# Feature-major float16 halves of both FFNs' routing: from TensorE transposes and two PSUM copies to transposing transfers on SyncE's queue

## The chip, the cores and the metric

The kernel runs on one NeuronCore of a Trainium2 chip. The metric is device time in microseconds (us) of one execution. The kernel before took 2360.64 us (median of three runs: 2363.73, 2360.64, 2348.91). Below, PE is TensorE, PEld its weight load, DVE is VectorE, ACT is ScalarE, POOL is GpSimd, and SP is SyncE, which computes nothing and issues transfers. "DMA share" is the mean busy share of the core's 16 DMA engines.

## The reference

The input `x` has 2 sequences of 4096 tokens with 512 features. Three layers follow one another: half an FFN, an attention layer with a delta-rule state, and the same FFN again with the same weights. Only the FFN's routing matters here:

```python
x = x + 0.5 * ffn(layernorm(x), ...)
x = x + attn(layernorm(x), ...)
x = x + 0.5 * ffn(layernorm(x), ...)

# ffn, on the normalised x
ctx = concatenate([x, broadcast(slot_mean)], axis=-1)
h = gelu(ctx @ w1.T + b1, approximate=False)            # 256 hidden features
route_logits = (h @ w2.T + b2) / (abs(tau) + 0.1)       # 64 slots
topk_vals, topk_idx = top_k(route_logits, 8)
alpha = softmax of the 8 kept logits, 0 elsewhere       # token x slot
slot_input = einsum('bts,btd->bsd', alpha, x)
...                                                     # a GRU step on the slots
out = einsum('bts,bsd->btd', alpha, slot_values) @ wo.T + bo
```

A product on PE contracts over partitions. So `ctx @ w1.T` needs the normalised `x` with features on the partitions (feature-major), while the layer norm makes it with tokens on the partitions, and the slot sum wants tokens on the partitions.

## The kernel before, in words

The program has five stretches: routing of the first FFN (phase "a", tiles whose names end in `a`), its GRU step, attention (the long middle), routing of the second FFN (phase "c"), and the last GRU step with the output. Both routings run the same function, `ffn_a_phase` (line 309).

A block is 128 tokens of both sequences (`NB` = 2, written `b`), so there are 32 blocks. Blocks are put in groups of four (the first, and the last few, in smaller ones). Each group goes through six generators, and `run_merged` (line 60) deals them out by a due time that each `yield` gives, in units of groups. The order that this makes is what the Tile framework starts from when it fixes each engine's own order; at run time each engine, SP among them, runs its instructions in that order and waits at one until what it depends on is done. The generators are:

- `a_load` (line 349) starts the load of a block's `x`, 512 KB, on SP's queue, 1.4 groups ahead. Phase a has 7 buffers `xt` for it, phase c has 4, and 12 blocks kept in tiles `kx` for the end.
- `a_stats` (line 355): mean and variance on DVE (`bn_stats`, line 361).
- `a_norm` (line 368): DVE writes the normalised block `fxn` (line 379, 2 buffers); ACT rounds it to float16, `xh` (line 383); POOL takes the rest, `xl = fxn - xh`, in float16 (line 385). The pair keeps the product close to float32. Then both halves are made feature-major: for each, PE makes 8 transposes of 128x128 (line 394, tile `fpt`) into a PSUM tile, and ACT (for `xh`, line 397) or DVE (for `xl`, line 399) copies that to `fxTh` or `fxTl` in SBUF, 3 buffers each. The PSUM tiles come from the pool `ptr` (tag `tr`, 3 buffers), which other users share.
- `a_hidden` (line 402), due 0.44 groups (1.76 blocks) after the norm of the same block: 24 matmuls on PE through `mm3` (lines 128 to 130: `fxTh` by the high half of w1, `fxTh` by its low half, `fxTl` by the high half), tile `fph`, then Gelu on ACT (line 417, tile `hT`) and the logits on PE (line 421, tile `pl`).
- `a_topk` (line 425), once for a group, nearly all on DVE: the eight largest logits, the softmax, and the two float16 halves `ahl` of alpha.
- `a_slots` (line 463): PE transposes alpha (tile `fpa`, line 472), ACT copies it out (line 579 in phase a, from where SP stores it to `ald` at line 580; line 595 in phase c), and PE adds up the slots from `xh`, `xl` and `ahl` (lines 480 to 482, tile `sl`). So `xh` and `xl` stay alive until then (10 or 11 buffers).

Phase a also prepares attention's weights in between: their loads are on SP's queue, their splitting is on DVE and ACT (line 176 and 177), and 96 matmuls are on PE (line 248). SP's queue holds, in phase a, the loads `xt`, the weight loads and the stores `ald`; in phase c the loads of `xt` and `kx`, and the weights of the GRU step.

Of the kernel before, what the change touches and what calls it, by code (L numbers as in the profile page):

```python
# [11 lines left out]
F16 = mybir.dt.float16  # L12
# [7 lines left out]
P = 128  # L20
D = 512
KC = D // P
# [5 lines left out]
NB = 2  # L28
# [66 lines left out]
def tile_macaron(  # L95
# [7 lines left out]
    nc = tc.nc  # L103
    V = nc.vector
# [30 lines left out]
    ident16 = cp.tile([P, P], F16, tag="ident16", name="ident16")  # L135
# [173 lines left out]
    def ffn_a_phase(load, adst, nm, extra, before=None, after=None):  # L309

        with tc.tile_pool(name=f"sl{nm}", bufs=1, space=PSUM) as slp, tc.tile_pool(name=f"gp{nm}", bufs=1) as gp:
# [3 lines left out]
            with tc.tile_pool(name=f"f{nm}", bufs=2) as wp, tc.tile_pool(name=f"fs{nm}", bufs=2) as sm, \  # L315
                    tc.tile_pool(name=f"ft{nm}", bufs=3, space=PSUM) as ptr, \
                    tc.tile_pool(name=f"fp{nm}", bufs=2, space=PSUM) as ppj, \
                    tc.tile_pool(name=f"fl{nm}", bufs=2, space=PSUM) as ppl:
                groups = split_blocks(NBLK)
                ng = len(groups)  # L320
                pools = (wp, sm, ptr, ppj, ppl)
                st = [dict() for _ in range(ng)]
                items = []
                for g, (b0, n) in enumerate(groups):
                    args = (st[g], nm, g, (b0, n), pools)
                    t0, t1 = b0 / GB, (b0 + n) / GB
                    items += [
                        (t0 - PA["ld"] - n / GB, t1 - PA["ld"] - n / GB, lambda a=args: a_load(*a, load)),
                        (t0 - PA["st"], t0 - PA["st"] + PA["std"], lambda a=args: a_stats(*a)),
                        (t0, t1, lambda a=args: a_norm(*a)),  # L330
                        (t0 + PA["a2"], t1 + PA["a2"], lambda a=args: a_hidden(*a)),
                        (t1 + PA["a2"], t1 + PA["tk"], lambda a=args: a_topk(*a, wacc)),
                        (t1 + PA["tk"], t1 + PA["tk"] + PA["sl"] * n / GB, lambda a=args: a_slots(*a, adst, sl, ng)),
                    ]
                items += extra(gp, ptr, gw, NBLK / GB)
                run_merged(items)
                for i in range(1, GB):
                    nc.gpsimd.tensor_tensor(wacc[:, 0:NB], wacc[:, 0:NB], wacc[:, NB * i:NB * i + NB], ALU.add)
# [29 lines left out]
    def a_norm(d, nm, gi, blocks, pools):  # L368

        wp, sm, ptr, ppj, ppl = pools  # L370
        mv, rs = d["mv"], d["rs"]
        d["xhl"], d["xT"] = [], []
        for j in range(blocks[1]):
            u = f"{nm}{gi}_{j}"
            xs = d["x"][j]
            xn = wp.tile([P, NB, D], F32, tag="xn", name=f"fxn{u}", bufs=CFG[nm]["XN"])
            for b in range(NB):
                i = NB * j + b
                V.tensor_scalar(xn[:, b], xs[:, b], mv[:, i, 0:1], rs[:, i:i + 1], ALU.subtract, ALU.mult)
            xh = wp.tile([P, NB, D], F16, tag="xh16", name=f"xh{u}", bufs=CFG[nm]["XH"])  # L380
            xl = wp.tile([P, NB, D], F16, tag="xl16", name=f"xl{u}", bufs=CFG[nm]["XH"])
            d["xhl"].append((xh, xl))
            nc.scalar.copy(xh, xn)
            yield (j + 0.2) / blocks[1]
            nc.gpsimd.tensor_tensor(xl, xn, xh, ALU.subtract)
            yield (j + 0.4) / blocks[1]
            xTh = wp.tile([P, KC, NB * P], F16, tag="xTh", name=f"fxTh{u}", bufs=3)
            xTl = wp.tile([P, KC, NB * P], F16, tag="xTl", name=f"fxTl{u}", bufs=3)
            d["xT"].append((xTh, xTl))
            for src16, dst, eng in ((xh, xTh, 0), (xl, xTl, 1)):  # L390
                pt = ptr.tile([P, KC, NB * P], F16, tag="tr", name=f"fpt{u}_{eng}")
                for k in range(KC):
                    for b in range(NB):
                        nc.tensor.transpose(pt[:, k, b * P:(b + 1) * P], src16[:, b, k * P:(k + 1) * P], ident16)
                    yield (j + 0.4 + 0.3 * eng + 0.07 * (k + 1)) / blocks[1]
                if eng == 0:
                    nc.scalar.copy(dst, pt)
                else:
                    V.tensor_copy(dst, pt)
                yield (j + 0.7 + 0.3 * eng) / blocks[1]  # L400

    def a_hidden(d, nm, gi, blocks, pools):

# [764 lines left out]
```

## Time and profile before

One profiled execution took 2342.8 us, of which 2341.0 us are the span from its first instruction to its last, at a mean granted TensorE clock of 0.960. It is 18 us under the median of the three timed runs.

| what | value |
|---|---|
| DVE, busy of the span | 1911.3 us (82%) |
| ACT, busy of the span | 1148.9 us (49%) |
| POOL, busy of the span | 808.5 us (35%) |
| first and last `bn_stats` of phase a | 16.0 and 208.4 us |
| first transpose `fpt` and last slot matmul of phase a | 26.2 and 273.8 us |
| first transpose `fpt` and last slot matmul of phase c | 2019.6 and 2250.0 us |
| transfers issued by SP in phase a, one `xt` load | 512 KB, median 0.38 us of SP's time |

The engines' busy times lie side by side, so they are not added up. A stretch is set by the engine that is busy nearly all of it, or by a chain of waits where none is. How much an instruction costs is seen from its duration only on DVE, ACT and POOL; matmuls overlap in the pipeline, and what counts there is how far apart they start.

### The profile page before, as it was taken

The page shows a single profiled execution, that of the slowest core. Times are in us where ns is not written, and L with a number is a line of the kernel's source. Part 1 is how long each engine was busy: PE and PEld are TensorE (multiplying, and loading weights), DVE is VectorE, ACT ScalarE, POOL GpSimd, SP SyncE. Part 2 cuts the span into 40 slices and gives each one's busy share as a digit, 9 for nine tenths or more (in the row PEclk, how much of TensorE's full clock was granted, in tenths as well). Part 3 has the DMA queues.
Part 4 walks back from the last instruction along what each step waited for, and adds up shares of the span by engine and source line. Part 5 has one row for each costly group of instructions (what it writes and reads, how often), then busy time and mean ns, then how long its engine had stood idle before and what let it go on. Part 6 is the DMA issues. An engine that isn't in the chain of part 4 may idle for free. (4 is left out here: it accounts for less than half of the span.)

```text
span 2341.0 us, 101047 instructions
## 1 busy us (share of the span) xinstructions
PE 2100.5 (90%) x44989; PEld 1585.4 (68%) x44989; DVE 1911.3 (82%) x4876; ACT 1148.9 (49%) x1957; POOL 808.5 (35%) x750
## 2 busy tenths in 40 slices
PE   5878878999999999999999999999999976588886
PEld 5767757767777676777767677777667754377774
DVE  7898538988888888888889888888888886489656
ACT  4677445544445444444545444554444421367631
POOL 2333114433334343333434333444333441134300
PEclk9898989999999999999999999999999988799997
DMA  6332323344443344343334444344444332630049
GB/s 212 123 127 91 96 87 129 119 133 130 142 134 126 123 136 132 128 150 121 126 124 139 128 136 148 120 127 132 135 128 146 102 97 70 219 110 29 2 149 368
DMA packets 176516, 302.75 MB, mean 129 GB/s; under 512 B 27984, under 2 KB 73552, under 8 KB 176080
## 3 DMA queue, kind: packets, MB, share of 16 engines
q1 hardware_dynamic: 161728, 256.45, 32.9%
q10 hardware_dynamic: 14352, 39.85, 5.2%
q8 instruction: 352, 5.77, 1.2%
q14 instruction: 84, 0.69, 0.1%
HBM read 189.23 MB, written 107.00 MB: 127 GB/s over the span
## 5 line engine op out<-in xcount | busy, mean ns | idle before, releaser
L1080 PE MATMUL apo<-wo,Gt 128*128 128x512 f32 x512 | 279.1, 630 | 24.5 <-DVE x1r L1083 24.5
L128 PE MATMUL pv<-xTh,wgh 128*128 128x256 f16 x1024 | 282.1, 275 | 0.0
L129 PE MATMUL pv<-xTh,wgl 128*128 128x256 f16 x1024 | 280.2, 274 | 0.1
L130 PE MATMUL pv<-xTl,wgh 128*128 128x256 f16 x1024 | 280.3, 274 | 0.0
L1014 POOL TENSOR_TENSOR ps<-ST,AC 128x256 f32<-128x256 f32 x128 | 105.5, 824 | 442.4 <-DVE ST L1038 442.4
L128 PE MATMUL pq<-wqh,xTh 128*128 128x384 f16 (+1 forms) x768 | 242.8, 316 | 1.5 <-issue 0.8
L129 PE MATMUL pq<-wqh,xTl 128*128 128x384 f16 (+1 forms) x768 | 240.9, 314 | 0.2 <-DVE xTl L818 0.2
L130 PE MATMUL pq<-wql,xTh 128*128 128x384 f16 (+1 forms) x768 | 240.7, 313 | 0.0
L862 POOL TENSOR_TENSOR qk<-qk,rn 128x512 f32<-128x512 f32 x128 | 137.6, 1075 | 231.7 <-issue 106.7
L836 ACT ACTIVATE qk<-pq,iscA 128x384 f32<-128x384 f32 (+1 forms) x192 | 105.4, 549 | 162.5 <-PE pq L130 139.5
L980 POOL TENSOR_TENSOR KQ<-KQ,Ax 128x512 f32<-128x512 f32 x128 | 168.4, 1315 | 0.4 <-PE pa L959 0.4
L764 DVE TENSOR_TENSOR tmp<-N,MT 128x256 f32<-128x256 f32 (+7 forms) x384 | 161.2, 426 | 5.6
L758 DVE TENSOR_TENSOR tmp<-N,U 128x256 f32<-128x256 f32 (+7 forms) x384 | 164.0, 434 | 1.4
L838 ACT ACTIVATE sq<-pq,iscA 128x384 f32<-128x384 f32 (+1 forms) x192 | 164.7, 858 | 0.0
L1018 PEld LDWEIGHTS pc<-KQ,S 32*32 32x32 f32 x8192 | 123.2, 106 | 50.6 <-ACT Y L1044 31.0
L760 DVE TENSOR_REDUCE MT<-tmp 128x32 f32<-128x256 f32 (+7 forms) x384 | 153.8, 407 | 0.0
L959 PE MATMUL pa<-KQ 32*32 32x64 f32 x8192 | 143.6, 217 | 11.2 <-ACT KQ L872 4.9
L1018 PE MATMUL pc<-KQ,S 32*32 32x64 f32 x8192 | 142.8, 217 | 9.5 <-DVE S L1040 4.9
L959 PEld LDWEIGHTS pa<-KQ 32*32 32x32 f32 x8192 | 121.7, 105 | 37.9 <-issue 14.9
L1035 PEld LDWEIGHTS pc<-X,u 32*32 32x32 f32 x8192 | 120.7, 105 | 38.6 <-issue 21.9
L1035 PE MATMUL pc<-X,u 32*32 32x64 f32 x8192 | 141.9, 216 | 5.2 <-ACT u L1032 3.7
L917 ACT ACTIVATE vg<-pv,iscA 128x512 f32<-128x512 f32 x128 | 88.1, 688 | 96.7 <-PE pv L130 88.7
(304 smaller groups left out, 5760.3 us busy)
## 6 DMA issues: line engine op xcount, KB each, us to landing
d<-a0d ACTq DMA_DIRECT2D x32, 528.0 KB
Ax<-a0d ACTq DMA_DIRECT2D x32, 528.0 KB
xt<-in_x_dram SPq DMA_DIRECT2D x32, 512.0 KB
x<-in_x_dram SPq DMA_DIRECT2D x64, 256.0 KB
x1d<-x SPq DMA_DIRECT2D x64, 256.0 KB
vtd<-vg SPq DMA_DIRECT2D x64, 256.0 KB
kd<-qk SPq DMA_DIRECT2D x64, 256.0 KB
XK<-kd SPq DMA_DIRECT2D x256, 64.0 KB
```

The costliest lines, as they stand in the source:

```text
L128: nc.tensor.matmul(po, lh, rh, start=start, stop=False, skip_group_check=True)
L129: nc.tensor.matmul(po, ll, rh, start=False, stop=False, skip_group_check=True)
L130: nc.tensor.matmul(po, lh, rl, start=False, stop=stop, skip_group_check=True)
L758: V.tensor_tensor(tv, vw(f, o10 + j0, [[C, n], [0, h], [1, ni]]), vw(U, ou + j0 * 17, [[0, n], [16, h], [1, ni]]), ALU.mult)
L760: yield lambda tv=tv, j0=j0: V.tensor_reduce(vw(mt, n * j0, [[1, n], [n, h]]), tv, AX.X, ALU.add)
L764: V.tensor_tensor(tv, vw(f, o11 + r0 * C, [[C, h], [0, n], [1, nk]]), vw(mt, 0, [[0, h], [n, n], [1, nk]]), ALU.mult)
L838: nc.scalar.activation(sq[:, f0:f1].rearrange("p (q g e) -> p q e g", g=NG, e=C), pq[:, 0:f1 - f0].rearrange("p (q e g) -> p q e g", g=NG, ...
L959: nc.tensor.matmul(pa[s, m], KQ[s, 0, c, b, g], KQ[s, :, c, b, g], start=(m == 0), stop=True, skip_group_check=True, tile_position=(32 * q ...
L980: nc.gpsimd.tensor_tensor(kc, kc, bass.AP(Ax.tensor, Ax[:, :, c].offset, [list(a[0]), [1, 2], list(a[1]), [1, C]]), ALU.mult)
L1018: nc.tensor.matmul(pcv[s, b, g, 0:2 * C], S[s, b, g], KQ[s, :, c, b, g], start=(g == 0), stop=False, skip_group_check=True, tile_position=tp)
L1035: nc.tensor.matmul(pcv[s, b, g, C:3 * C], u[s, b, g], d["X"][s, :, m], start=False, stop=True, skip_group_check=True, tile_position=tp)
L1080: nc.tensor.matmul(po, Gt[:, k, b], wo[:, k], start=(k == 0), stop=(k == KC - 1))
```

## The change

In `a_norm`, the loop that makes a half feature-major no longer uses PE and PSUM. For each half and each of the two sequences, SP issues one transposing transfer from the token-major half (128 partitions of 512 float16 values, 128 KB) to the feature-major tile (128 partitions, 4 runs of 128 values). A block takes four of them. The due times within the block are kept at the points where the copies stood; the four yields between the transposes of a half are gone. Nothing else is changed: the tiles, their buffers and the matmuls that read them are the same. It holds for both phases.

```diff
             xTh = wp.tile([P, KC, NB * P], F16, tag="xTh", name=f"fxTh{u}", bufs=3)
             xTl = wp.tile([P, KC, NB * P], F16, tag="xTl", name=f"fxTl{u}", bufs=3)
             d["xT"].append((xTh, xTl))
-            for src16, dst, eng in ((xh, xTh, 0), (xl, xTl, 1)):
-                pt = ptr.tile([P, KC, NB * P], F16, tag="tr", name=f"fpt{u}_{eng}")
-                for k in range(KC):
-                    for b in range(NB):
-                        nc.tensor.transpose(pt[:, k, b * P:(b + 1) * P], src16[:, b, k * P:(k + 1) * P], ident16)
-                    yield (j + 0.4 + 0.3 * eng + 0.07 * (k + 1)) / blocks[1]
-                if eng == 0:
-                    nc.scalar.copy(dst, pt)
-                else:
-                    V.tensor_copy(dst, pt)
-                yield (j + 0.7 + 0.3 * eng) / blocks[1]
+            for src16, dst, i in ((xh, xTh, 0), (xl, xTl, 1)):
+                for b in range(NB):
+                    nc.sync.dma_start_transpose(dst[:, :, b * P:(b + 1) * P], src16[:, b])
+                yield (j + 0.7 + 0.3 * i) / blocks[1]
```

## The prediction, made before the changed kernel ran

> **What bounds the kernel now.** I read the page's summary first, and cut it down: the edit touches two stretches, the routings. Their transposes run from 26 to 256 us and from 2020 to 2231 us of a span of 2341.0 us, so four fifths of the program, attention, is untouched. Next I asked for the busy times of the engines in six windows of each routing. Columns: window, length, busy PE, PEld, DVE, ACT, POOL (with instruction counts), granted PE clock, DMA share, GB/s.
>
> ```profile
> 26.00:66.00 40.00, 37.90 (x384) 34.95 (x385) 34.58 (x93) 27.18 (x35) 18.19 (x10) 1.00 0.64 192
> 66.00:106.00 40.00, 32.03 (x353) 27.77 (x350) 35.22 (x98) 25.15 (x35) 12.04 (x7) 0.87 0.34 114
> 106.00:146.00 40.00, 31.45 (x365) 27.79 (x365) 38.59 (x92) 30.95 (x49) 14.25 (x7) 0.91 0.26 81
> 146.00:186.00 40.00, 29.59 (x329) 26.10 (x329) 39.18 (x96) 24.20 (x36) 11.35 (x6) 0.83 0.38 131
> 186.00:226.00 40.00, 33.48 (x448) 30.42 (x447) 32.26 (x78) 31.59 (x47) 15.59 (x8) 0.91 0.30 100
> 226.00:266.00 40.00, 37.39 (x489) 33.69 (x488) 25.18 (x93) 24.09 (x36) 9.00 (x5) 0.91 0.11 38
> ```
>
> ```profile
> 2020.00:2056.00 36.00, 28.77 (x266) 24.03 (x264) 23.00 (x56) 23.29 (x30) 12.94 (x8) 0.83 0.76 277
> 2056.00:2092.00 36.00, 30.03 (x326) 26.14 (x327) 30.20 (x75) 22.13 (x31) 13.83 (x7) 0.86 0.28 94
> 2092.00:2128.00 36.00, 31.24 (x402) 27.28 (x398) 32.97 (x111) 26.55 (x36) 10.86 (x6) 1.00 0.18 60
> 2128.00:2164.00 36.00, 27.73 (x342) 24.33 (x343) 33.42 (x89) 26.44 (x37) 17.86 (x9) 0.95 0.00 1
> 2164.00:2200.00 36.00, 29.64 (x418) 27.21 (x417) 27.68 (x68) 27.95 (x38) 17.56 (x9) 0.95 0.01 2
> 2200.00:2241.00 41.00, 38.18 (x513) 34.43 (x513) 26.29 (x94) 25.18 (x37) 6.88 (x4) 0.96 0.01 2
> ```
>
> The reader is to see three things. In the middle of phase a DVE is the limit (38.6 and 39.2 of 40 us). At the ends of both phases PE is (37.9, 37.4 of 40; 38.2 of 41). Elsewhere PE and DVE are both at 75 to 92%, waiting for each other in turn. The DMA engines are busy early and idle late: lengths times shares add up to 81 us in phase a and 45 us in phase c.
>
> Third, the transposes' own share of those windows, asked by their tile. The first sum is phase a's 240 us, the second phase c's 221 us; columns PE, DVE, ACT.
>
> ```profile
> sum 240.00, PE 62.13 DVE 21.95 ACT 32.32; mean PE 10.35 DVE 3.66 ACT 5.39
> ```
>
> ```profile
> sum 221.00, PE 56.57 DVE 21.67 ACT 32.35; mean PE 9.43 DVE 3.61 ACT 5.39
> ```
>
> Last, who waits for whom (us in total, times, longest), in phase a. DVE, a limiting engine, sits idle before its own copy until PE has transposed; the matmuls hardly wait for that copy.
>
> ```profile
> DVE fxTla L399 <- PE fpta L394: 15.4, 7, 8.1
> ...
> PE fpha L130 <- DVE fxTla L399: 4.9, 4, 3.5
> ```
>
> **What goes.** PE loses 512 transposes a phase. One lasts 219 ns, but they start some 0.11 us apart, so the busy time that is only theirs is the count: 62.1 and 56.6 us. ACT loses 32 copies of 1.01 us in each phase. DVE loses 32 copies of 0.68 us, 22.0 and 21.7 us. Two PSUM tiles a block go; the trace shows 0.7 us of waiting for them, so that is costed at nothing. Where DVE is near its limit its copies come off the time one for one; where PE is, the time falls until DVE or a chain stops it.
>
> One end of the gain: the busier engine sets each window and the window shrinks with it. Taking the transposes' part per window off both (11.94 us of PE and 4.11 of DVE in the first, and so on), the six of phase a become 32.2, 36.1, 36.4, 36.5, 33.7 and 29.4 us (40 x 30.5/37.9 for the first), a gain of 36 us; those of phase c give 39. Together 75 us. The other end: DVE's copies count only in the second to fourth window of each phase, where DVE is the busiest, 10 and 11 us, 21 us together. I take all of DVE's copies and nothing for PE, 22.0 + 21.7 = 44 us, because DVE is the busiest engine or within a tenth of it in nine of the twelve windows, and the time that PE gives up beyond that will partly turn into waits for the transfers.
>
> **What comes.** 128 transposing transfers of 131072 bytes a phase, 256 in all, 33.6 MB. The trace has none, so the price is bounded by the queue's row.
>
> ```profile
> q1 hardware_dynamic: 161728, 256.45, 32.9%
> ```
>
> 32.9% of 2341 us is 770 us for 256.45 MB: 333 GB/s, or 4.76 ns for a packet over the 16 engines, 1586 bytes on average. At that rate a transfer takes 0.39 us; less is excluded, since the bytes are the same. If it goes by packets and one is a partition's 256-byte run of 128 values, it has 512 and takes 2.44 us. The nearest row is that of plain transfers whose source is, as here, 1 KB on each of 128 partitions: 128 packets, 0.61 us. I take 0.61, so 78 us a phase. With the 81 and 45 us already there the DMA engines are at 159 of 240 us and 123 of 221: beside other work, not the limit. The price at which they become the limit is (240 - 81)/128 = 1.24 us in phase a and (221 - 45)/128 = 1.38 us in phase c. Below it the cover holds; above it each further 0.1 us costs 26 us.
>
> The Trainium skill has two rules here that disagree. "DMA: Bandwidth & Descriptors", section "Latency and other measured facts", gives a transposing transfer 261 GB/s with a non-contiguous middle dimension; an estimate from that is 0.50 us for a transfer, which keeps the sum as it is. "VectorE: DVE Perf Modes", section "The three transpose paths", speaks against the change: 1309 ns for 128x128 by DMA against 390 ns by TensorE, and use TensorE where PSUM will do. Taken as a cost for each of the four squares of a transfer, an estimate of 5.2 us each, it would make both phases some 700 us long and the kernel some 1000 us slower; taken as a delay that overlaps, it changes little. The trace has PE's 219 ns (0.11 apart) in place of 390 and nothing on the other number.
>
> **SP's queue.** A plain issue takes SP some 0.4 us, so four of them 1.6 us of a block's 7 us; SP waits over 200 us of phase a and stands idle for the last 136 us of phase c (its last load is issued at 2114). New is that SP waits for `xh` (ACT) and `xl` (POOL) before it issues. Queued behind that wait are the next loads `xt`, for which `bn_stats` on DVE waits (1.1 us in phase a, 9.5 in phase c now), weight loads, and the stores `ald`, which nobody needs before attention. Loads are due 5.6 blocks ahead of the norm, and the last of a group about one block (7 us) before its statistics, so a stall of SP under that costs nothing; beyond it each group of four pays the excess once. The other way round, the transfers stand behind SP's waits for free `xt` buffers (49 us in phase a, 82 in c) and on the rings behind bulk loads (512 KB at 333 GB/s is 1.6 us; four weights of 2 to 3 MB are 6 to 9 us each).
>
> **The new wait on the path.** `fph`'s matmuls now wait for a transfer. From `xl` on there were transposes (16 x 0.11) and a copy (0.7): about 2.5 us, plus DVE's queue. Now there are four issues (1.6), transfers (4 x 0.61, partly beside them) and a landing delay; the only row for that is a reader of the stored `hsd` that waited 4.7 us under an early DMA share of 0.8. So 3 to 8 us. The order leaves 1.06 blocks, about 7.5 us, between issue and first reader. That cover is enough late and thin early: I give 3 us to the start of each phase, taken from PE's uncounted part. Behind the waiting matmul on PE stand the logits and slot sums of older blocks.
>
> **Rivals.**
> Transfers too dear (slower): the one mechanism is a price over 1.24 to 1.38 us for each 128 KB, when the DMA engines become the bound. At 2.44 us the phases need 128 x 2.44 + 81 = 393 us and 357 us, 153 + 136 = 289 us more: 2342.8 + 289 = 2632. For it: data are cut into short runs somewhere. Against: the queue's plain rate leaves a factor of three.
> Waits instead of work (about the same, or a little slower): blocks take turns with the transfers in flight, `bufs=3` being held longer. If each of the 64 blocks loses 0.7 us the 44 us are gone: 2343. If each loses 1.5 us, the time is +52: 2395. For it: DMA share 0.64 and 0.76 in the first windows, and the thin cover. Against: no transfers at all late in phase c.
> More than forecast (faster): PE's whole 119 us come off, 2224. Against it: DVE alone keeps 205 - 22 = 183 us of work in phase a, and this would make that phase's 240 us 178.
> That the edit does not remove PE's transposes can be excluded: the loop is gone.
>
> **How the numbers follow.** Against the profiled 2342.8 us the forecast is 2342.8 - 44 = 2299; the same 44 off the median 2360.64 gives 2317. Its own range, 75 to 21 us, is 2286 to 2340. About 1%, 24 us, is what a measurement of this kernel tells from no change. Chances: forecast 0.49; more than forecast 0.05; waits that eat it 0.13; waits that cost more 0.12; transfers too dear 0.21. So faster 0.54, same 0.13, slower 0.33. The range starts a little under the forecast's end, at 2280, and must reach into the dear transfers: at 1.93 us they cost 160 us, 2520. Left out are the dearer ones and part of the large gain, together under 2 in 10.
>
> **What will show it.** In the changed profile PE's and ACT's `fpt` groups are gone and the DMA queue carries 33.6 MB more; the growth of its time, over 256, is the price (right near 0.6, wrong over 1.2). DVE's 15.4 us wait is gone, and `fph` waiting for `fxTl` shows the new wait in total (right under 20 us a phase). The last slot matmul of phase a ends near 252 instead of 274 us. If `bn_stats` waits for `xt` by tens of us, SP's order has failed; if DMA shares are at 0.9 through both routings, the price has.

## The result and the profile after

The changed kernel took 2366.28 us (median of ten runs, 2360.69 to 2373.87), the one before 2353.60 us in ten runs. The ratio is 1.0049, 95% interval 1.0029 to 1.0069: half a per cent slower, beyond the interval, and within the 1% that the prediction called the same. 2317 us had been forecast. Slow executions are left out of every ratio here; the only one, of 4919.84 us, was of the version with unattended transfers below. The profiled execution took 2366.12 us, with a span of 2364.3 us, 23.3 us more than the span before.

First the parts. The attention stretch between its first and last store of its output was 1525.0 us before and 1534.3 us after, and it lies between 1525 and 1535 us in all the profiles of this study, with the same code; so a single span can't be read more closely than that, and the routings are read from their own marks. Phase a's last slot matmul starts at 299.9 us in place of 273.8: 26 us later. From attention's last store to phase c's last slot matmul it was 2002.6 to 2250.0, 247 us, and is 2038.8 to 2276.5, 238 us: 10 us shorter.

Next the windows of phase a in the changed kernel, with the columns as before (window, length, busy PE, PEld, DVE, ACT, POOL, granted clock, DMA share, GB/s):

```profile
26.00:66.00 40.00, 28.17 (x147) 23.71 (x148) 23.23 (x63) 13.74 (x17) 17.48 (x9) 0.74 0.72 170
66.00:106.00 40.00, 32.91 (x250) 27.79 (x248) 21.20 (x67) 16.54 (x23) 7.71 (x4) 0.80 0.76 181
106.00:146.00 40.00, 26.41 (x299) 23.14 (x297) 29.38 (x80) 21.52 (x34) 9.73 (x5) 0.84 0.70 162
146.00:186.00 40.00, 28.97 (x309) 25.09 (x306) 34.11 (x91) 23.18 (x40) 12.53 (x6) 0.81 0.69 147
186.00:226.00 40.00, 26.28 (x271) 22.64 (x269) 31.73 (x87) 21.84 (x35) 10.28 (x5) 0.83 0.78 184
226.00:266.00 40.00, 30.43 (x299) 25.54 (x298) 34.11 (x79) 26.14 (x36) 17.58 (x9) 0.79 0.75 178
```

No engine is busy any more where one always was: DVE had 38.6 and 39.2 us in the third and fourth window and has 29.4 and 34.1; PE had 37.9 and 37.4 in the first and last and has 28.2 and 30.4. The DMA engines are at 0.7 to 0.8 and not at their limit either. What they wait for shows among the waits of phase a (engine, tile and line waited for: us in total, times, longest):

```profile
PE fpha L130 <- DMA fxTla<-xla: 28.8, 15, 6.0
...
DVE sta L361 <- DMA xt<-in_x_dram: 18.1, 7, 5.4
...
PE pgh L248 <- DMA whht<-in_whh_dram: 10.5, 4, 7.2
...
PE fpha L128 <- DMA fxTha<-xha: 9.0, 5, 4.9
```

and of phase c:

```profile
PE fphc L130 <- DMA fxTlc<-xlc: 32.9, 23, 3.3
...
DVE stc L361 <- DMA xt<-x2d: 25.5, 7, 9.4
...
PE fphc L128 <- DMA fxThc<-xhc: 11.2, 6, 4.3
```

In phase a PE waits 38 us for the transposed halves, and transfers that the change did not touch are late too: the loads of x (1.1 us of waiting before) and of a GRU weight. All were issued by SP. Its timeline near the start of phase a (start, length, engine, line, operation, count):

```profile
54.53 2.50 SPq L392 DMA_TRANSPOSE fxTla<-xla  x2
57.13 2.52 SPq L392 DMA_TRANSPOSE fxTha<-xha  x2
59.74 0.53 SPq L556 DMA_DIRECT2D xt<-in_x_dram  x1
60.38 2.50 SPq L392 DMA_TRANSPOSE fxTla<-xla  x2
```

SP issues one after the other with 0.1 us between them, and a transposing issue takes it 1.25 us, where a plain load takes 0.53. Over the phase:

```profile
L392 SPq DMA_TRANSPOSE fxTha<-xha x64: 1194/1252/3142, 26.2 to 277.4; - x64
L392 SPq DMA_TRANSPOSE fxTla<-xla x64: 1188/1251/4178, 28.8 to 280.0; - x64
```

(ns: shortest, median, longest; then first and last start in us.) 128 issues at 1.25 us are 160 us of the 255 us that they span, before SP has issued anything else. With the loads and stores in between, the issues take 207 of these 255 us, 81%, and 184 of 205 us, 90%, in phase c (sums over the trace). The bytes are the forecast's, and their price on the DMA engines is to be seen in the queue's row:

```profile
q1 hardware_dynamic: 300992, 290.04, 40.8%
```

33.6 MB more; 40.8% of 2364.3 us less 32.9% of 2341.0 us is 194 us, 0.76 us for each of the 256 transfers.

### The profile page after: what moved, and what is told of

Its sections match the earlier page's. It is cut to its first block, busy times and chain, and to the rows that moved or that the text cites. A ratio compares the mean times of both kernels' runs of the same rounds, so it can differ in the third digit from the quotient of the medians.

```text
span 2364.3 us, 99310 instructions
## 1 busy us (share of the span) xinstructions
PE 2069.6 (88%) x43965; PEld 1540.2 (65%) x43965; DVE 1868.5 (79%) x4812; ACT 1081.6 (46%) x1886; POOL 806.4 (34%) x750
## 3 DMA queue, kind: packets, MB, share of 16 engines
q1 hardware_dynamic: 300992, 290.04, 40.8%
## 4 chain that ended last, share of the span: by engine, by line
PE 58%; DMA 10%; DVE 10%; SPq 3%; issue 3%; ACT 1%; POOL 1%; DVEq 0%; ACTq 0%; POOLq 0%
PE apo L1073 9%; PE pa L952 5%; PE pv L128 5%; PE pc L1028 5%; PE pc L1011 4%; PE pv L130 4%; PE pv L129 4%; PE pq L128 4%; DMA kd<-qk 4%; PE pq L129 4%; PE pq L130 4%; PE pc L1021 3%; DMA x1r<-x1d 2%; PE kqt L862 2%; SPq L392 2%
## 5 line engine op out<-in xcount | busy, mean ns | idle before, releaser
L759 DVE TENSOR_REDUCE N<-tmp 128x32 f32<-128x128 f32 (+4 forms) x320 | 135.5, 423 | 0.0
```

## The experiments

Each was timed beside the kernel before; a ratio is to that. The difference of two ratios is uncertain by some 0.0035, or 8 us, as their intervals say. The framework plans each engine's order anew for each kernel, so an edit can also move work that it does not name.

**What the removed work was worth.** The halves of a phase's first block serve for all of its blocks:

```diff
+            first = nm not in once
+            if first:
+                once[nm] = (wp.tile(..., tag="xTh", bufs=1), wp.tile(..., tag="xTl", bufs=1))
+            xTh, xTl = once[nm]
...
+                if first:
                     for b in range(NB):
                         nc.sync.dma_start_transpose(dst[:, :, b * P:(b + 1) * P], src16[:, b])
```

> The feature-major halves of a phase's first block are made by transposing transfers and then read by all 32 blocks; no other block is transposed, so the routing is computed from the wrong tokens. Nothing else changes. It measures what the removed work was worth with nothing put in its place. Theory (the removal is worth what was forecast, and the new transfers give it back): DVE's copies come off at least, 44 to 75 us, so 2280 to 2310 us. Rival (the transposes and copies lay beside other work, and there was little to gain): 2340 to 2354 us.

Measured: 2292.36 us, ratio 0.9732 (0.9706 to 0.9759), 63 us less than before. Phase a's last slot matmul starts at 245.1 us, 29 us earlier. The theory holds: removing the transposes and copies is worth more than the 44 us taken, inside the 21 to 75 us given. The gain was there and was given back. The 63 us may hold a little more than the work, though: here the matmuls need not wait for the norm of their own block either.

**The transfers without the waits for them.** The same, and the other blocks' transposing transfers are issued into tiles that nobody reads:

```diff
+            xd = [wp.tile([P, KC, NB * P], F16, tag="xd", name=f"fxd{u}_{i}", bufs=DB) for i in range(2)]
...
+                else:
+                    for b in range(NB):
+                        nc.sync.dma_start_transpose(xd[i][:, :, b * P:(b + 1) * P], src16[:, b])
```

> As e1_no_transposes, but SP also issues all the transposing transfers of the change, into tiles that nothing reads (4 buffers for each block's two halves in turn). So SP's queue and the DMA engines are loaded as in the changed kernel, but no matmul waits for a transfer. Theory A (SP's queue and the DMA engines are what costs: 1.25 us of SP for each of 256 issues, with the loads of x and of the weights queued behind them): 2340 to 2366 us, near the changed kernel. Theory B (the matmuls' wait for the landed transfer is what costs, 30 to 40 us a phase in the changed kernel's waits): within 15 us of e1_no_transposes.

Measured: 2341.61 us, 0.9941 (0.9915 to 0.9967), 49 us over the kernel without transposes, as theory A has it. So two thirds of what was given back is paid although no instruction reads the result, and the remaining 25 us (1.0049 less 0.9941) come of the matmuls' waiting for their own block's halves. This tells SP and DMA engines from waits; the next ones tell SP from the DMA engines.

**The same bytes in half the issues, unattended.**

```diff
-                    for b in range(NB):
-                        nc.sync.dma_start_transpose(xd[i][:, :, b * P:(b + 1) * P], src16[:, b])
+                    nc.sync.dma_start_transpose(xd[i], flat(src16))
```

> As e2_unattended, with one unattended transposing transfer of 256 KB for each half in place of two of 128 KB: the same bytes by the crossbar, half the issues on SP, nothing waits for them. Theory (SP's queue: 1.23 us an issue, whatever its size): of the 49 us that the unattended transfers cost, more than half goes, 2305 to 2322 us. Rival (the DMA engines' time for the bytes): 2330 to 2345 us, as e2_unattended.

Measured: 2301.59 us, 0.9774 (0.9752 to 0.9797). A little under the theory's range: of the 49 us, 39 are gone (0.9941 less 0.9774) while the queue moves as much, as its row on the page shows:

```profile
q1 hardware_dynamic: 297024, 290.02, 42.5%
```

and its unattended issues of high halves in phase a (ns: shortest, median, longest):

```profile
L402 SPq DMA_TRANSPOSE fxda<-xha x31: 1231/1255/3819, 31.6 to 234.1; - x31
```

An issue of 256 KB takes SP the same 1.25 us as one of 128 KB. All the bytes on the DMA engines, and two issues a block, cost 10 us. In phase a SP's issues take 69% of the time between its first and last transposing one, where with four issues a block they took 86%.

**The changed kernel with half the issues, attended.** This is a working version:

```diff
-            xTh = wp.tile([P, KC, NB * P], F16, tag="xTh", name=f"fxTh{u}", bufs=3)
-            xTl = wp.tile([P, KC, NB * P], F16, tag="xTl", name=f"fxTl{u}", bufs=3)
+            xTh = wp.tile([P, NB, KC, P], F16, tag="xTh", name=f"fxTh{u}", bufs=3)
+            xTl = wp.tile([P, NB, KC, P], F16, tag="xTl", name=f"fxTl{u}", bufs=3)
...
-                for b in range(NB):
-                    nc.sync.dma_start_transpose(dst[:, :, b * P:(b + 1) * P], src16[:, b])
+                nc.sync.dma_start_transpose(dst.rearrange("p b k t -> p (b k) t"), flat(src16))
...
-                    mm3(ph[:, hc], ..., xTh[:, k], xTl[:, k], k == 0, k == KC - 1)
+                    mm3(ph[:, hc].rearrange("p (b t) -> p b t", b=NB), ..., xTh[:, :, k], xTl[:, :, k], k == 0, k == KC - 1)
```

> The changed kernel with one transposing transfer of 256 KB for each half in place of two of 128 KB; the feature-major tiles are kept as sequence, feature chunk, token for it, and the matmuls read two runs of 128 tokens. Two issues a block in place of four, the same bytes. Theory A1 (SP's 1.25 us is a price for each issue): it stays near 1.25, SP has 2.5 us less to do in each block, and some 20 to 40 us come back, 2325 to 2345 us. Theory A2 (it is a price for what is moved): an issue takes some 2.5 us and the time stays within 10 us of the changed kernel's 2366.

Measured: 2326.60 us, 0.9860 (0.9831 to 0.9889): 40 us under the changed kernel (44 by the ratios), and faster than the kernel before. A1 holds and A2 falls. The waits shrink with it, in phase a:

```profile
PE fpha L130 <- DMA fxTla<-xla: 11.8, 9, 2.3
...
DVE sta L361 <- DMA xt<-in_x_dram: 6.9, 3, 4.4
```

The DMA share is higher here, not lower: 1.01 from 66 to 106 us, where the changed kernel had 0.76. Late issues had kept the DMA engines from their work; in that window of this version the engines are full, so there the bytes may be the limit.

**Twice the issues.** Each transfer cut in two by its source partitions:

```diff
                 for b in range(NB):
-                    nc.sync.dma_start_transpose(dst[:, :, b * P:(b + 1) * P], src16[:, b])
+                    for h in range(2):
+                        r = slice(64 * h, 64 * h + 64)
+                        nc.sync.dma_start_transpose(dst[:, :, b * P + 64 * h:b * P + 64 * h + 64], src16[r, b])
```

> The changed kernel with each transposing transfer cut in two by its source partitions (0 to 63, 64 to 127): eight issues of 64 KB a block, the same bytes. Theory (SP's queue): at 1.23 us an issue SP needs 8 x 1.23 = 9.8 us a block for these alone, more than the 7.5 us that a block takes, so a phase takes at least 32 x 10 = 320 us and the kernel 2440 to 2540 us. Rival (bytes and packets on the DMA engines): 2360 to 2390 us.

Measured: 2667.19 us, 1.1322 (1.1301 to 1.1343), even more than SP's arithmetic gave, and why it is more stays open: phase a's last slot matmul starts at 446 us, and phase c takes 394 us in place of 238. SP's timeline in phase a is full, one block after another:

```profile
113.87 5.21 SPq L394 DMA_TRANSPOSE fxTha<-xha  x4
119.19 5.06 SPq L394 DMA_TRANSPOSE fxTla<-xla  x4
124.29 0.58 SPq L558 DMA_DIRECT2D xt<-in_x_dram  x1
124.97 5.05 SPq L394 DMA_TRANSPOSE fxTha<-xha  x4
130.13 5.05 SPq L394 DMA_TRANSPOSE fxTla<-xla  x4
135.23 0.58 SPq L558 DMA_DIRECT2D xt<-in_x_dram  x1
```

Eight issues of 64 KB and one load take 11 us, the pace of a block in this stretch. Over the phase a block takes 12.5 us, and SP's issues fill 90% of the time. And the DMA engines, with the same bytes, are half idle, as a window shows:

```profile
106.00:186.00 80.00, 43.40 (x317) 33.26 (x316) 34.79 (x101) 22.76 (x33) 9.72 (x5) 0.69 0.49 117
```

Three working kernels move the same bytes with two, four and eight issues a block, and take 2327, 2366 and 2667 us.

**Plain transfers in their place.** The unattended transfers as plain copies of the same bytes in 256-byte runs:

```diff
-                        nc.sync.dma_start_transpose(xd[i][:, :, b * P:(b + 1) * P], src16[:, b])
+                        nc.sync.dma_start(xd[i][:, :, b * P:(b + 1) * P], src16[:, b].rearrange("p (k t) -> p k t", k=KC))
```

> As e2_unattended, with each unattended transposing transfer replaced by a plain transfer of the same 128 KB to the same place, in the same runs of 256 bytes; still nothing reads them. Theory A (SP's 1.25 us): a plain issue of some 0.4 us leaves SP free, and the time falls from e2_unattended's 2342 to e1_no_transposes' 2292 or a little over, up to 2310 us. Rival (the DMA engines' time for 512 small packets): it stays at 2325 to 2342 us.

Measured: 2324.28 us, 0.9853 (0.9826 to 0.9881). Between the two expectations. SP's price for one is 0.63 us (median), not the 0.4 assumed: four of them are as much of SP as two transposing ones, yet this costs 28 us over no transfers (0.9853 less 0.9732) and those cost 10. Phase a alone goes by SP's time: its last slot matmul starts at 257.9 us here, at 256.9 with two transposing issues a block and at 282.2 with four. The rest of the difference lies behind it, 8 us in phase c and 11 us between phase a and attention's first store, and what makes it was not separated. The time on the DMA engines speaks against being it: 0.61 us for each of these by the queue's row, 1.6 for a transposing one of 256 KB.

**More buffers**, for both feature-major tiles of phase a:

```diff
-            xTh = wp.tile([P, KC, NB * P], F16, tag="xTh", name=f"fxTh{u}", bufs=3)
+            xTh = wp.tile([P, KC, NB * P], F16, tag="xTh", name=f"fxTh{u}", bufs=5 if nm == "a" else 3)
```

> The changed kernel with five buffers in place of three for each feature-major tile in phase a; phase c as it was. Theory (SP's queue is late, and more buffers do not make it issue faster): phase a ends within 8 us of the changed kernel's 300 us, 2355 to 2370 us. Rival (three buffers are too few for transfers in flight): phase a ends before 285 us, 2335 to 2350 us.

Measured: 2362.93 us, 1.0028 (1.0008 to 1.0047). Phase a's last slot matmul starts at 294.0 us, against 299.9, and the wait is the same:

```profile
PE fpha L130 <- DMA fxTla<-xla: 28.3, 14, 5.4
```

Three buffers were not what held the transfers back in phase a.

**Loads on another queue**, and likewise x in phase c, the stores of alpha and four weights:

```diff
-        nc.sync.dma_start(xt, xr[t * P:(t + 1) * P])
+        nc.gpsimd.dma_start(xt, xr[t * P:(t + 1) * P])
```

> The changed kernel with the loads of x, the stores of alpha and the four weight loads of the routings issued on GpSimd's queue; SP keeps the transposing transfers. The same bytes move. Theory (in the one queue of SP, loads stand behind transposing issues and their waits, and these behind the loads): the waits of bn_stats for x (18 and 26 us) and of the w_hh products for their weights (10 us) go, 2335 to 2352 us. Rival (the DMA engines hold them back, whichever queue issues): 2360 to 2370 us.

Measured: 2407.32 us, 1.0206 (1.0175 to 1.0237): both expectations miss. Phase a ends as in the changed kernel (301.2 us), though there `bn_stats` waits only 1.8 us for x and no longer 18; phase c takes 268 us in place of 238. In phase c the loads wait for a free buffer on POOL, and the low half that POOL computes stands behind them:

```profile
POOL xt L595 <- DVE fxnc L379: 65.3, 12, 17.2
```

The edit put new waits where it took one away, so whether the loads' place behind the transposing issues matters by itself stays open.

**One half only.** High halves on PE and ACT, low halves by transfers; and the other way round, with `i == 0`:

```diff
+                if i == 1:
+                    for b in range(NB):
+                        nc.sync.dma_start_transpose(dst[:, :, b * P:(b + 1) * P], src16[:, b])
+                    yield (j + 0.7 + 0.3 * i) / blocks[1]
+                    continue
                 pt = ptr.tile([P, KC, NB * P], F16, tag="tr", name=f"fpt{u}_{i}")
...
```

> Half of the change: the low halves come by transposing transfers, the high halves as before by TensorE and ScalarE's copy. DVE's 64 copies go, 512 of 1024 transposes stay, and SP has two transposing issues a block in place of four (2.5 us of some 7). Theory A (SP's queue full): under the limit of the queue DVE's 22 us a phase become time, 2315 to 2335 us. Theory B (the landing wait of the low half): the wait stays, since the low half is the late one, 2350 to 2366 us.

> The other half of the change: the high halves come by transposing transfers, the low halves as before by TensorE and DVE's copy. ScalarE's 64 copies go, DVE's stay. Theory A (SP's queue full): the queue is as free as in e3_xl_only, but DVE keeps its copies and only PE's 30 us a phase and ACT's 32 are gone, 2335 to 2354 us. Theory B (the landing wait of the low half): the low half is no transfer here, so there is no such wait, and the time falls as far as PE's part allows, 2320 to 2340 us, below e3_xl_only.

Measured: low half 2323.58 us, 0.9867 (0.9839 to 0.9895); high half 2343.19 us, 0.9952 (0.9933 to 0.9971). Theory A gave both ranges, theory B had the order the wrong way round. Both have two issues a block and lose half of the transposes. The one that frees DVE of its copies (44 us) gains 31 us, the one that frees ACT, off the limit, of its copies (65 us) gains 11.

And the low half in one transfer for both sequences, with its tile and the matmuls that read it laid out for that:

```diff
-                    for b in range(NB):
-                        nc.sync.dma_start_transpose(dst[:, :, b * P:(b + 1) * P], src16[:, b])
+                    nc.sync.dma_start_transpose(dst.rearrange("p b k t -> p (b k) t"), flat(src16))
```

> e3_xl_only with the low half of both sequences in one transposing transfer: one issue a block. Theory A1 (price for each issue): a little below e3_xl_only's 2324, 2308 to 2320 us. Theory A2 (price for what is moved): the same as e3_xl_only within 5 us.

Measured: 2321.76 us, 0.9842 (0.9817 to 0.9867). An issue stays at 1.23 us, as theory A1 says, but its range was missed, and the time is the one that A2 gave: the interval overlaps that of the two-issue version. From two issues to one nothing measurable is gained, where from four to two some 40 us were. With two, SP's issues take 58% of phase a's stretch, and what is saved there is no longer time.

**A version under both.** Low half only in phase a, both halves in phase c, where fewer other transfers run, one transfer for each half.

```diff
+                if i == 0 and nm == "a":
+                    pt = ptr.tile([P, NB, KC, P], F16, tag="tr", name=f"fpt{u}_{i}")
...
+                    nc.scalar.copy(dst, pt)
+                    yield (j + 0.7 + 0.3 * i) / blocks[1]
+                    continue
+                nc.sync.dma_start_transpose(dst.rearrange("p b k t -> p (b k) t"), flat(src16))
```

> In phase a only the low half goes by transposing transfers, in phase c both halves, always one transfer of 256 KB for a half. By the phases of the profiles so far, a as short as in e8_xl_one (end at 262 us) and c as short as in e5_one_per_half (224 us from the last store of attention to the last slot matmul): 2310 to 2322 us, under both. If the phases hang together in another way: no better than e8_xl_one's 2322.

Measured: 2309.16 us, 0.9803 (0.9783 to 0.9824), 2% faster than the kernel before, 1 us under the expected range and the fastest working version here. Phase a's last slot matmul starts at 266.8 us; from attention's last store (1999.5) to phase c's (2219.6) it is 220 us.

## Why the prediction was wrong

- **What goes: the mechanism held, the size was a little low.** 44 us were taken, 21 to 75 given; without the work and without a replacement 63 us go. One reading behind it does not hold: in phase c's first window neither PE (28.8 of 36 us) nor DVE (23.0) is at its limit.
- **The price on the DMA engines: right.** 0.61 us taken, 0.39 to 2.44 given, 0.76 measured, under the 1.24 and 1.38 at which they would become the limit. The rival of too dear transfers did not come. The Trainium skill, "DMA: Bandwidth & Descriptors", section "Latency and other measured facts", has 261 GB/s for this; 131072 bytes in 0.76 us are 172 GB/s here. That is still near enough for that step; a price of 5.2 us, worked out from the other page's 1309 ns for each square, does not occur.
- **SP's queue: the step that failed.** It said "A plain issue takes SP some 0.4 us, so four of them 1.6 us of a block's 7 us". A transposing issue takes 1.25 us, so four are 5.0 us. The operation was not in the trace, its transfer was bounded from both sides, but its issue was priced by another kind of instruction and given no upper end. So SP had 3.4 us more to do in each block than the sum held; taking 2.5 us of them away, from four unattended issues to two, gave 39 us.
- A rule of the skill would have supported the same slip: "DMA: Bandwidth & Descriptors", section "Issuing engines are not separate DMA queues", says that the time a sequencer takes to start a transfer is usually small beside the transfer. Here the issue (1.25 us) is longer than the transfer's share of the DMA engines (0.76 us), and the measurement decides.
- **The new wait: right in place, low in size.** 3 us a phase were allowed; `fph` waits 29 + 9 us in phase a and 33 + 11 in phase c, and 25 us of time come of it. The 29 and 33 us for `fxTl` are over the bound set beforehand, 20 us a phase. What failed is the cover: the order was to leave about 7.5 us between issue and first reader, but from the end of a block's last low-half issue to the first matmul that reads it the trace has a median of 2.9 us in phase a and 1.6 us in phase c, because SP is late. Matmuls that waited for it started 1.3 us (median) after that end. With half the issues the cover is 5.0 and 5.9 us, and the waits shrink. But the attended kernel still lies 20 us over its unattended twin (0.9860 less 0.9774), whose matmuls wait for nothing of their block, not even its norm; how much of these 20 us is the landing was not separated.
- **The rival that came** is the one of waits, which had 2343 to 2395 us and 0.25. Its reason, three buffers held longer, was wrong in phase a: with five the wait was the same, and the kernel's time within the noise. The sign that was named for SP's order having failed, `bn_stats` waiting for x by tens of us, is there, 18 and 26 us. Phase a's last slot matmul, due near 252 us, starts at 299.9.
- The sum, in ratios to before: the work removed, -0.0268; the DMA engines and two issues, +0.0042; the other two issues, +0.0167; the matmuls' wait for their own block's halves, +0.0108. Together +0.0049. These are differences between one version and the next, so they must add up to the result and do not check it.

## What to carry to other kernels

Price the issue of a transfer as its own instruction on the queue's engine, apart from the bytes, and bound it from both sides when its kind is not in the trace; a queue in order has a pace for each block like any other engine. A late queue also eats the cover of whoever reads what it brings. Where issues and not bytes are the limit, make fewer and larger ones: the same change with one transfer for a half is 1.4% faster than the kernel before, where with two it is 0.5% slower. Take first what frees the busiest engine (here DVE's copy); the half whose copy is off the limit can stay where it was.

## What the hardware showed that was not expected

- A transposing issue took SP 1.25 us for 64, 128 and 256 KB alike (medians 1.246, 1.252, 1.251), a plain one 0.32 to 0.53, a plain one in 256-byte runs 0.63. The share of the DMA engines goes by bytes: 0.36, 0.76 and 1.60 us, each from the growth of the queue's time over the number of transfers.
- The queue's packets grew by 288, 544 and 1056 for these sizes: 512 for 128 KB, and 32 for each issue.
- PE, busy for 173 us and not 202 of the 240 us from 26 to 266 us, was granted a lower clock: 0.77, 0.82 and 0.81 in their three stretches of 80 us, against 0.94, 0.87 and 0.91 before, and the hidden layer's matmuls took 308 ns on average, not 288. The Trainium skill, "TensorE: Matmul & The Clock Gate", section "What's actually happening", has the clock released by recent activity and throttled without it, which agrees. How much of the time this cost was not tested by itself.
